# Sorting and summing graph edges in eight column groups, with the stages of neighbouring groups side by side

## The chip, the cores and the metric

The kernel runs on one core of a Trainium2 chip. The metric is device time in microseconds; the kernel before took 3344.22 us (median of three runs, 3344.13 to 3344.76). Less is better.

The engines named here are PE (matrix products), DVE (elementwise work and reductions), ACT (activation functions, copies), POOL (which issues the indirect transfers) and SP (which issues plain transfers). PEld is PE's weight load. ACT can issue plain transfers too.

## The reference

There are 6250 nodes with 128 features and 206250 edges with 128 features. Each edge row is added to its source node; then a small network runs on every node, and a layer norm closes it:

```python
row = edge_index[0]                       # the source node of every edge
edge_aggr = jnp.zeros((n, HIDDEN)).at[row].add(edge_features)
global_expand = jnp.repeat(global_feat, reps, axis=0)
combined = jnp.concatenate([x, edge_aggr, global_expand], axis=-1) @ W_c + b_c
h = jax.nn.softplus(combined @ W1 + b1)
h = jax.nn.softplus(h @ W2 + b2)
return _layernorm(x + (h @ W3 + b3), axis=-1)
```

The source indices come in no useful order, so the sum is a scatter with repeated targets. All values are float32.

## The kernel before

**Layout.** Nodes are cut into blocks of 128; with a node for indices out of range there are `NB` = 49 blocks. Edges are held as 128 partitions by `TC` = 1612 columns: partition p has 1611 consecutive edges, and column 1611 holds the last 42. A bucketed row in DRAM is 129 floats (516 B): the 128 features, and the node's place within its block.

**Sort.** DVE turns the indices into block and place (L126 to L144). For each of the 49 blocks one operation over all columns marks the edges of that block and counts them by partition (L150). Products with a triangle and with ones give each partition's base and the totals (L154, L156). A bucket is padded to whole superchunks of 256 rows. Rows behind the buckets are zeroed by 14 plain transfers (L118) and by 98 indirect ones of 128 rows each (L210, called for `zeros`). Positions follow in groups of 90 columns: a running sum for each block and a predicated copy (L233, L235), then a conversion to integers (L237).

**Scatter.** Nine columns of edge rows at a time are loaded by SP into one of four buffers (L242), ACT adds the place within the block as column 129 (L245), and POOL issues one indirect transfer for each column of 128 rows (L210). There are 1612 of them, into one DRAM tensor `bucketed`.

**Sums.** The sums read `bucketed`, so they begin when every scatter has landed. SP loads eight superchunks at a time (L285). For each 128 rows DVE makes a one-hot matrix (L295) and PE multiplies (L297); after both halves of a superchunk DVE adds the product to the transposed sums at an offset read from `offs` (L300). Each matrix product in float32 shows as two instructions.

**Network.** For 512 nodes at a time: products on PE, softplus in three steps on ACT and two on DVE, the residual, the norm, and the store.

The order of the work on each engine is the framework's: it schedules the instructions by the program's order and by what is ready. The scatters are declared free of order among themselves.

Of the kernel before, what the change touches and what calls it, by code (L numbers as in the profile page):

```python
# [10 lines left out]
U8 = mybir.dt.uint8  # L11
# [7 lines left out]
GROUP_COLS = 90  # L19
SUB = 2  # L20
SC = SUB * P
SC_PER_LOAD = 8
EPS = 1e-5


@with_exitstack
def kernel(
# [24 lines left out]
    # Node N stands for indices out of range, and is no row of the result.  # L52
# [3 lines left out]
    NSC = (E + NB * (SC - 1)) // SC  # L56
    ROWS = NSC * SC
    W = D + 1

    const = ctx.enter_context(tc.tile_pool(name="const", bufs=1))  # L60

# [1 line left out]
    iota_f = const.tile([P, P], F32, name="iota_f")  # L63
    nc.gpsimd.iota(iota_f, pattern=[[1, P]], base=0, channel_multiplier=0,
# [4 lines left out]
    ident = const.tile([P, P], F32, name="ident")  # L69
    nc.vector.tensor_scalar(ident, iota_f, part_f, None, op0=ALU.is_equal)  # L70
    after = const.tile([P, P], F32, name="after")
    nc.vector.tensor_scalar(after, iota_f, part_f, None, op0=ALU.is_gt)
    ones = const.tile([P, P], F32, name="ones")
    nc.vector.memset(ones, 1.0)

    offs = const.tile([1, NSC], I32, name="offs")
    sums_t = const.tile([P, NB * P], F32, name="sums_t")
    nc.gpsimd.memset(sums_t, 0.0)

# [1 line left out]
    wc_sb = const.tile([P, 3, D], F32, name="wc_sb")  # L81
    nc.scalar.dma_start(wc_sb, w_c.rearrange("(k p) d -> p k d", p=P))
    w_sb = {}
    for name, w in (("w1", w1), ("w2", w2), ("w3", w3)):
        w_sb[name] = const.tile([P, D], F32, name=f"{name}_sb")
        nc.scalar.dma_start(w_sb[name], w)
    cols = const.tile([P, 4], F32, name="cols")
    for i, v in enumerate((b_c, b1, b2, global_feat.rearrange("o d -> (o d)"))):
        nc.scalar.dma_start(cols[:, i:i + 1], v.rearrange("(p o) -> p o", o=1))
    b3_row = const.tile([1, D], F32, name="b3_row")  # L90
    nc.scalar.dma_start(b3_row, b3.rearrange("(o d) -> o d", o=1))
    c_bias = const.tile([P, 1], F32, name="c_bias")

    dram = ctx.enter_context(tc.tile_pool(name="dram", bufs=1, space=bass.MemoryType.DRAM))
    bucketed = dram.tile([ROWS + NB * SUB * P, W], F32, name="bucketed")

# [1 line left out]
    with ExitStack() as phase:  # L98
        keep = phase.enter_context(tc.tile_pool(name="keep", bufs=1))
        scans = phase.enter_context(tc.tile_pool(name="scans", bufs=2))  # L100
        rows_p = phase.enter_context(tc.tile_pool(name="rows", bufs=4))
# [3 lines left out]
        if R:  # L105
            nc.vector.memset(src_i[:, T:TC], 0)
        nc.sync.dma_start(src_i[:, :T], src[:P * T].rearrange("(p t) -> p t", p=P))
        if R:
            nc.sync.dma_start(src_i[:R, T:TC], src[P * T:].rearrange("(p o) -> p o", o=1))

        # Rows past the last superchunk that is certainly used.
        ZR = 7
        zeros = keep.tile([P, ZR * W], F32, name="zeros")
        nc.gpsimd.memset(zeros, 0.0)
        tail = (NSC - NB) * SC
        for r0 in range(tail, ROWS, P * ZR):
            k = min(ZR, (ROWS - r0) // P)
            nc.sync.dma_start(  # L118
                bucketed[r0:r0 + P * k, :].rearrange("(p k) c -> p (k c)", p=P),
                zeros[:, :k * W],  # L120
            )

        # Negative indices count from the end; what is out of range goes to node N.
        node = keep.tile([P, TC], F32, name="node", tag="t0")
        wrap = keep.tile([P, TC], F32, name="wrap", tag="t1")
        nc.vector.tensor_copy(node, src_i)  # L126
        nc.vector.tensor_scalar(wrap, node, 0.0, float(N), op0=ALU.is_lt, op1=ALU.mult)
        nc.vector.tensor_add(node, node, wrap)
        nc.vector.tensor_scalar(node, node, -1.0, float(N), op0=ALU.max, op1=ALU.min)
        nc.vector.tensor_scalar(wrap, node, 0.0, float(N + 1), op0=ALU.is_lt, op1=ALU.mult)  # L130
        nc.vector.tensor_add(src_i, node, wrap)
        part_i = keep.tile([P, TC], I32, name="part_i", tag="t1")
        block = keep.tile([P, TC], BF16, name="block")
        nc.vector.tensor_scalar(part_i, src_i, 7, None, op0=ALU.arith_shift_right)
        nc.vector.tensor_copy(block, part_i)
        if R:
            # The last column has R edges.
            none = keep.tile([P, 1], F32, name="none")
# [86 lines left out]
        while g0 < TC:  # L225
            g1 = min(TC, g0 + GROUP_COLS)
            if TC - g1 <= 1:
                g1 = TC
# [158 lines left out]
```

## Time and profile before

| | |
|---|---|
| median of the runs | 3344.22 us |
| span of the profiled execution | 3156.7 us |
| own time of that execution | not listed apart from its span; the runs' median stands for it |
| POOL busy | 1695.3 us (54%) |
| DVE busy | 1161.0 us (37%) |
| PE busy | 716.9 us (23%) |
| ACT busy | 178.2 us (6%) |
| bytes moved | 346.72 MB, 110 GB/s on the mean |

The span runs from the first to the last instruction; the rest of the time lies around it. A profile row of the groups gives line, engine, operation, tiles, shapes and count, then the busy time, the mean duration in ns, and the idle time ahead of it with what ended it. Timeline rows begin with the start and the length in us. A row of a window gives start and end, the length, each engine's busy time with its number of instructions, then PE's granted clock, the mean busy share of the 16 DMA engines and what they moved.

### The profile page before, as it was taken

To read this page: it belongs to the slowest core of one execution; us is meant where nothing else is said; L and a number is where in the kernel's file an instruction comes from. 1 tells how busy PE (TensorE), PEld (TensorE's weight loads), DVE (VectorE), ACT (ScalarE), POOL (GpSimd) and SP (SyncE) were. 2 spreads that over 40 slices of the span, in tenths; PEclk is the share of its full clock that TensorE was granted. 3 is DMA by queue.
4 is the path that set the end of the run, shared out by engine and by line. 5 is a ranking of instruction groups with operands and counts; after the bars stand their busy time and mean duration, and the time that the engine had idled before them with its cause. 6 is when DMAs were issued, how large, how long until landed. Compare 5 with 4: busy or idle time off the path is not lost. (4 is left out here: it accounts for less than half of the span.)

```text
span 3156.7 us, 18596 instructions
## 1 busy us (share of the span) xinstructions
PE 716.9 (23%) x3776; PEld 527.9 (17%) x3776; DVE 1161.0 (37%) x4793; ACT 178.2 (6%) x368; POOL 1695.3 (54%) x1720
## 2 busy tenths in 40 slices
PE   0000000000000000000000000000049999999885
PEld 0000000000000000000000000000037777777543
DVE  9999995000000000000000000000029999999644
ACT  0000000000000000000000000000000000000267
POOL 1577777777777777777777777777730000000000
PEclk9999999999999999999999999999999999999965
DMA  3012333333333333333333333333356565656200
GB/s 128 15 48 71 97 98 103 103 101 104 104 105 105 104 105 104 105 105 105 104 105 104 105 105 105 104 103 102 102 156 188 176 187 177 185 178 185 68 16 24
DMA packets 386717, 346.72 MB, mean 110 GB/s; under 512 B 33101, under 2 KB 355802, under 8 KB 386602
## 3 DMA queue, kind: packets, MB, share of 16 engines
q1 hardware_dynamic: 328812, 228.93, 25.8%
q0 software_dynamic: 54720, 113.01, 11.0%
q10 hardware_dynamic: 3070, 3.60, 0.4%
q14 instruction: 85, 0.70, 0.1%
q8 instruction: 30, 0.49, 0.1%
HBM read 222.83 MB, written 122.57 MB: 109 GB/s over the span
## 5 line engine op out<-in xcount | busy, mean ns | idle before, releaser
L210 POOL DMA_INDIRECT bucketed<-rows,pos x1612 | 1562.0, 969 | 491.6 <-issue 489.4
L297 PE MATMUL part<-hot,chunks 128*128 128x128 f32 x3416 | 569.9, 302 | 2273.1 <-DVE hot L295 2246.5
L295 DVE TENSOR_SCALAR hot<-iota_f,chunks 128x128 f32<-128x128 f32 x1708 | 406.7, 280 | 1818.5 <-DMA chunks<-bucketed 1812.8
L297 PEld LDWEIGHTS part<-hot,chunks 128*128 128x128 f32 x3416 | 448.2, 191 | 2394.1 <-issue 2213.6
L233 DVE TENSOR_TENSOR_SCAN scan<-ones,scan,in_block 128x90 f32<-128x90 f32 (+1 forms) x833 | 323.1, 389 | 0.0
L300 DVE TENSOR_TENSOR sums_t<-sums_t,part 128x128 f32 x854 | 245.4, 287 | 63.2 <-PE part L297 34.9
L235 DVE COPY_PREDICATED pos_f<-in_block,scan 128x90 f32<-128x90 uint8 (+1 forms) x882 | 200.0, 228 | 0.0
L210 POOL DMA_INDIRECT bucketed<-zeros,pad_i x98 | 124.0, 1266 | 132.5 <-DVE pos_f L235 103.3
L245 ACT COPY rows<-low 128x9 f32<-128x9 f32 x179 | 36.6, 206 | 2230.0 <-DMA bucketed<-rows,pos 2219.4
L150 DVE TENSOR_SCALAR_CACHE_REDUCE in_block<-block 128x1612 uint8<-128x1612 bf16 x49 | 85.9, 1821 | 0.0
L329 ACT ACTIVATE comb<-comb_ps,c_bias 128x512 f32<-128x512 f32 (+1 forms) x13 | 8.4, 646 | 617.4 <-PE comb_ps L326 617.4
L340 PE MATMUL y_ps<-w_sb,h 128*128 128x128 f32 (+1 forms) x98 | 33.2, 437 | 26.1 <-DVE h L313 25.6
L341 PE MATMUL y_ps<-b_row,ones 1*128 1x128 f32 (+1 forms) x98 | 35.6, 459 | 0.0
L340 PEld LDWEIGHTS y_ps<-w_sb,h 128*128 128x128 f32 (+1 forms) x98 | 24.6, 291 | 53.5 <-DVE h L313 36.4
L310 ACT ACT_TABLE_LOAD x26 | 33.4, 1283 | 0.5
L313 DVE TENSOR_TENSOR h<-h,away 128x512 f32<-128x512 f32 (+1 forms) x26 | 17.1, 656 | 37.5 <-ACT away L310 37.5
L318 PE MATMUL z_ps<-h,w_sb 128*128 128x512 f32 (+1 forms) x26 | 22.8, 976 | 9.3 <-DVE h L313 9.3
L154 PE MATMUL before_ps<-count,after 128*128 128x49 f32 x2 | 0.7, 432 | 106.7 <-DVE in_block L150 106.7
L342 DVE TENSOR_TENSOR y<-y_ps,x_sb 128x128 f32<-128x128 f32 (+1 forms) x49 | 13.8, 285 | 29.6 <-PE y_ps L341 29.6
L309 ACT ACT_TABLE_LOAD x19 | 24.4, 1283 | 0.3
L341 PEld LDWEIGHTS y_ps<-b_row,ones 1*128 1x128 f32 (+1 forms) x98 | 22.1, 279 | 9.9 <-issue 8.5
L312 DVE TENSOR_SCALAR h<-z_ps,cols 128x512 f32<-128x512 f32 (+1 forms) x26 | 18.2, 707 | 14.7 <-ACT away L308 14.7
(85 smaller groups left out, 284.8 us busy)
## 6 DMA issues: line engine op xcount, KB each, us to landing
chunks<-bucketed SPq DMA_DIRECT2D x106, 1032.0 KB, 5.3
rows<-in_edge_attr SPq DMA_DIRECT2D x179, 576.0 KB, 4.6
bucketed<-rows,pos POOLq DMA_INDIRECT x1612, 2.4
bucketed<-zeros SPq DMA_DIRECT2D x14, 451.5 KB, 8.7
out<-y SPq DMA_DIRECT2D x12, 256.0 KB, 2.2
bucketed<-zeros,pad_i POOLq DMA_INDIRECT x98, 2.4
src_i<-in_src SPq DMA_DIRECT2D x1, 805.5 KB
chunks<-bucketed SPq DMA_DIRECT2D x1, 774.0 KB
```

The lines of the kernel that those rows point to most:

```text
L150: nc.vector.tensor_scalar(in_block[:, b, :], block, float(b), None, op0=ALU.is_equal, op1=ALU.add, accum_out=count[:, b:b + 1])
L210: s = nc.gpsimd.indirect_dma_start(out=bucketed[:, :], out_offset=bass.IndirectOffsetOnAxis(ap=index, axis=0), in_=rows, in_offset=None)
L233: nc.vector.tensor_tensor_scan(scan[:, b, :n], ones[:, :n], in_block[:, b, g0:g1], first, op0=ALU.mult, op1=ALU.add)
L235: nc.vector.copy_predicated(pos_f[:, g0:g1], in_block[:, b, g0:g1], scan[:, b, :n])
L245: nc.scalar.copy(rows[:, :k, D:W], low[:, c0:c0 + k].unsqueeze(2))
L295: nc.vector.tensor_scalar(hot, iota_f, chunks[:, s, j, D:W], None, op0=ALU.is_equal)
L297: nc.tensor.matmul(part, chunks[:, s, j, :D], hot, start=(j == 0), stop=(j == SUB - 1))
L300: nc.vector.tensor_add(here, here, part)
L309: nc.scalar.activation(away[:, :w], away[:, :w], AF.Exp, scale=-1.0)
L310: nc.scalar.activation(away[:, :w], away[:, :w], AF.Ln, bias=ones[:, :1])
L340: nc.tensor.matmul(y_ps[:r, :], h2[:, q0:q0 + r], w_sb["w3"], start=True, stop=False)
L341: nc.tensor.matmul(y_ps[:r, :], ones[:1, :r], b3_row, start=False, stop=True)
```

## The change

The 1612 columns are cut into eight groups of 64, 192, 384, 384, 288, 144, 92 and 64 columns. Each group has its own counts, positions, buckets and offsets. Buckets are padded to 128 rows (groups 0, 6 and 7) or to 256 (the others).

Three DRAM tensors, `places`, take the buckets: group 0 has its own, and the others alternate between two. Each tensor is filled once with -1; a row's last column now holds `1 + 128 * group + place in block`, so that a row left by an earlier group or by the fill matches no node of the present one. The indirect transfers of zero rows are gone.

In the main loop, for each group: its scatters, the positions of the next group, and the sums of the group before are written out in turn, piece by piece, and the order on PE, DVE, ACT and SP is the written one. Edge rows are loaded through ACT's queue three pieces ahead, into one of five buffers. Fills, row transfers for the positions, chunk loads and x go through SP's queue.

Positions are found in another way: a comparison of all columns of a part with all blocks at once in bfloat16; counts by products with ones; the base of each column as a bfloat16 pair of high and low byte, moved from partitions into one row by SP; a product with a triangle plus a product with the base row; then a multiplication by the comparison and a reduction over the 49 blocks. The one-hot matrices for 1024 rows are made by one operation, on rows loaded 1024 at a time. The MLP loads x again on ACT's queue, 512 nodes at a time; the transposes of x lie in the loop, in group 2.

The core of the diff:

```diff
+GROUPS = ((64, 1), (192, 2), (384, 2), (384, 2), (288, 2), (144, 2), (92, 1), (64, 1))
+CHUNK_ROWS = 1024
+FILL = 12
+POS_COLS = 8
+ROW_COLS = 64
...
+    rows_of = [nsc * sub * P for _, _, sub, nsc in groups]
+    place_rows = [rows_of[0]] + [max(rows_of[1 + i::2], default=0) for i in range(2)]
+    places = [dram.tile([r, W], F32, name=f"place{i}") for i, r in enumerate(place_rows) if r]
+    place_of = [0 if g == 0 else 1 + (g - 1) % 2 for g in range(G)]
...
+        rows_p = phase.enter_context(tc.tile_pool(name="rows", bufs=5))
+        chunks_p = phase.enter_context(tc.tile_pool(name="chunks", bufs=4))
+        hots = phase.enter_context(tc.tile_pool(name="hots", bufs=2))
...
+        def fill_rows(place, r0, r1):
+            for r in range(r0, r1, P * FILL):
+                k = min(FILL, (r1 - r) // P)
                 nc.sync.dma_start(
+                    places[place][r:r + P * k, :].rearrange("(p k) c -> p (k c)", p=P),
+                    fill[:, :k * W])
...
+            def count(k):
+                a, b = parts[k]
+                n = b - a
+                ib = hots_p.tile([P, P, NB], BF16, name="ib")
+                in_block[k] = ib
+                nc.vector.tensor_tensor(
+                    ib[:, :n, :], block[:, a:b].unsqueeze(2).to_broadcast([P, n, NB]),
+                    iota_h[:, :NB].unsqueeze(1).to_broadcast([P, n, NB]), op=ALU.is_equal)
+
+            def count2(k):
+                n = parts[k][1] - parts[k][0]
+                n_ps = ps.tile([P, NB], F32, name="n_ps")
+                for b in range(NB):
+                    nc.tensor.matmul(n_ps[:n, b:b + 1], in_block[k][:, :n, b], ones_h[:, :1],
+                                     start=True, stop=True)
+                nc.scalar.copy(n_all[:n, k, :], n_ps[:n, :])
...
+            def one_row(k, r0):
+                r1 = min(parts[k][1] - parts[k][0], r0 + ROW_COLS)
+                row = per.tile([2, ROW_COLS * NB], BF16, name="gb_row")
+                gb_row[k, r0] = row
+                for h in range(2):
+                    nc.sync.dma_start(row[h:h + 1, :(r1 - r0) * NB], got[k][r0:r1, h, :])
+
+            def place(k, j0, j1):
...
+                nc.tensor.matmul(pr[:, :m * NB], after_h, ib, start=True, stop=False)
+                r0 = j0 // ROW_COLS * ROW_COLS
+                nc.tensor.matmul(pr[:, :m * NB], scale_h,
+                                 gb_row[k, r0][:, (j0 - r0) * NB:(j1 - r0) * NB],
+                                 start=False, stop=True)
...
+            def place2(k, j0, j1):
...
+                nc.vector.tensor_mul(at[:, :m * NB], pr[:, :m * NB], ib)
...
+                    nc.vector.tensor_reduce(
+                        pos[:, a - c0 + j0:a - c0 + j1],
+                        at[:, :m * NB].rearrange("p (g b) -> p g b", b=NB),
+                        axis=mybir.AxisListType.X, op=ALU.add)
...
+            def load(i):
...
+                nc.sync.dma_start(
+                    t[:, :k * sub].rearrange("p (s j) c -> p s (j c)", j=sub),
+                    src_rows[s * sub * P:(s + k) * sub * P, :].rearrange(
+                        "(s p j) c -> p s (j c)", p=P, j=sub))
+
+            def match(i):
...
+                nc.vector.tensor_tensor(
+                    hot[:, :m], chunks[i][:, :m, D:W].to_broadcast([P, m, P]),
+                    code.unsqueeze(1).to_broadcast([P, m, P]), op=ALU.is_equal)
+
+            def total(i):
...
+                for s in range(k):
+                    part = ps.tile([P, P], F32, name="part", bufs=3)
+                    for j in range(sub):
+                        nc.tensor.matmul(part, t[:, s * sub + j, :D], hot[:, s * sub + j],
+                                         start=(j == 0), stop=(j == sub - 1))
+                    here = sums_t[:, bass.ds(at[s], P)]
+                    nc.vector.tensor_add(here, here, part)
...
+        with tc.manual_schedule(engines={ET.PE, ET.DVE, ET.Activation, ET.SP}):
...
+            fill_rows(0, 0, rows_of[0])
...
+            for step in positions(0):
+                step()
+            if G > 1:
+                fill_rows(1, 0, rows_of[1])
...
+            for g in range(G):
+                mine = [q for q in range(len(pieces)) if pieces[q][0] == g]
+                prep = positions(g + 1) if g + 1 < G else []
+                sums = reduce_steps(g - 1) if g else []
+                other = node_rows() if g == min(2, G - 1) else []
+                if g == 0 and G > 2:
+                    fill_rows(1, rows_of[1], place_rows[1])
+                if g == 1 and G > 2:
+                    fill_rows(2, 0, place_rows[2])
+                done = [0, 0, 0]
+                for q in mine:
+                    load_rows(i + 3)
+                    code_rows(i + 2)
+                    scatter_rows(i)
...
+                    for w, (todo, s) in enumerate(((prep, min(1.0, share * 1.15)), (sums, share),
+                                                   (other, share))):
+                        upto = int(round(len(todo) * s))
+                        for step in todo[done[w]:upto]:
+                            step()
+                        done[w] = upto
+            for step in reduce_steps(G - 1):
+                step()
...
+        x_sb = node_rows_of(work, nc.scalar, n0, w)
```

More of the change, by code (lines that the diff above doesn't have):

```diff
@@ L87 @@
     cols = const.tile([P, 4], F32, name="cols")
[L88 to L89 removed]
     b3_row = const.tile([1, D], F32, name="b3_row")
[L91 to L95, printed above, removed]
+    x_t = const.tile([P, N], F32, name="x_t")
@@ L114 @@
[L114 to L127, printed above, removed]
@@ L209, in scatter @@
-        def scatter(rows, index):
-            s = nc.gpsimd.indirect_dma_start(
-                out=bucketed[:, :], out_offset=bass.IndirectOffsetOnAxis(ap=index, axis=0),
-                in_=rows, in_offset=None)
-            tc.declare_no_dep(s.ins, group="scatter", reason="no two edges have one position")
-            tc.add_to_no_dep_group("scatter", s.ins)
-        for b in range(NB):
-            for k in range(SUB):
-                scatter(zeros[:, :W], pad_i[:, b, k:k + 1])
-        pos_f = keep.tile([P, TC], F32, name="pos_f", tag="t0")
```

454 lines of the change are left out of this document (284 added, 170 removed).

## The prediction

> **What bounds the kernel now.** I read the page's slices first, then busy times in windows cut at the stage borders, then the timeline at those borders. From the page:
>
> ```profile
> span 3156.7 us, 18596 instructions
> ...
> DVE  9999995000000000000000000000029999999644
> ...
> POOL 1577777777777777777777777777730000000000
> ...
> L210 POOL DMA_INDIRECT bucketed<-rows,pos x1612 | 1562.0, 969 | 491.6 <-issue 489.4
> ```
>
> POOL works alone in the middle, DVE (with PE) before and after: three stages in a row. The windows price them (columns: window, length, busy time and count of PE, weight loads, DVE, ACT, POOL, clock, DMA share, GB/s):
>
> ```profile
> 0.00:36.00 36.00, 0.00 (x0) 0.00 (x0) 29.57 (x34) 1.79 (x5) 9.26 (x10) 1.00 0.84 280
> 36.00:112.00 76.00, 3.02 (x7) 1.29 (x8) 74.54 (x103) 0.00 (x0) 0.00 (x0) 1.00 0.00 0
> 112.00:267.00 155.00, 2.10 (x5) 0.63 (x3) 154.78 (x674) 0.00 (x0) 124.26 (x99) 1.00 0.13 42
> 267.00:520.00 253.00, 0.00 (x0) 0.00 (x0) 251.92 (x1110) 4.13 (x20) 196.60 (x186) 1.00 0.34 96
> 520.00:2321.00 1801.00, 0.00 (x0) 0.00 (x0) 0.00 (x0) 32.16 (x156) 1365.20 (x1427) 1.00 0.36 103
> 2321.00:2334.00 13.00, 5.80 (x28) 5.83 (x29) 4.82 (x22) 0.02 (x1) 0.00 (x0) 1.00 0.92 270
> 2334.00:2969.00 635.00, 572.46 (x3443) 449.88 (x3442) 562.48 (x2540) 7.07 (x13) 0.00 (x0) 0.99 0.59 178
> 2969.00:3157.00 188.00, 133.51 (x299) 70.30 (x297) 82.91 (x313) 132.99 (x173) 0.00 (x0) 0.64 0.06 17
> ```
>
> 112 us of indices and counts, 155 us of padding scatters, 2054 us (267 to 2321) of 1612 edge scatters, 648 us of sums (2321 to 2969), 188 us of MLP. A scatter starts every 1801/1427 = 1.262 us while DVE rests and every 253/186 = 1.360 us beside a full DVE. Its gap is "issue": POOL waits for nothing, so its own work per scatter is the pace.
>
> **The sum's frame.** Outside the span lie 3344.2 - 3156.7 = 187.5 us, taken from the median, since the execution shown has no time but its span; the three runs lie within 0.6 us, so it matters little. I keep that part unchanged.
>
> **What stays on the path.** All 1612 edge scatters stay on POOL, one after another. Removed: the 98 padding scatters (155 us) and most of the 112 us ahead of them. Moved beside the scatters: sums of seven groups and positions of seven groups. Left behind the last scatter: sums of group 7, then the MLP.
>
> **First scatter: 33 us.** A group's place has (columns*128 + 49*(128*sub - 1))/(128*sub) chunks; group 0, with 64 columns and sub 1, has 112, that is 14336 rows of 516 B, 7.4 MB of filling. The nearest row for fills, and those for the small operations:
>
> ```profile
> 25.00:30.00 5.00, 0.00 (x0) 0.00 (x0) 5.00 (x7) 0.00 (x0) 0.00 (x0) 1.00 1.02 395
> ```
> ```profile
> L204 PEld LDWEIGHTS ended<-chunk_f,ones 49*1 49x1 f32 x4 | 0.3, 101 | 2.8 <-issue 1.5 <-DVE chunk_f L200 1.3
> L128 DVE TENSOR_TENSOR node<-node,wrap 128x1612 f32<-128x1612 f32 x1 | 1.8, 1836 | 0.0
> L188 DVE TENSOR_TENSOR spare<-spare,pad_f 128x98 f32<-128x98 f32 x1 | 0.3, 253 | 0.0
> ```
> ```profile
> 6.13 1.95 DVE L126 CAST node<-src_i 128x1612 f32<-128x1612 int32 x1 [5.12 <-DMA src_i<-in_src]
> ...
> 107.12 0.63 PE L156 MATMUL total_ps<-count,ones 128*128 128x49 f32 x2
> ...
> 109.58 0.19 DVE L172 SCALAR_TENSOR_TENSOR base<-start,before_ps 128x49 f32<-128x49 f32 x1
> ```
>
> Fill, indices and first rows, some 10 MB at 395 GB/s, take 25 us; issue and start bring them to about 30. In parallel: indices at 6 us, eleven small DVE operations at about 0.2 (between L188's 0.25 and overlap) 2.5, the comparison of 64*49 = 3136 elements at 1836/1612 = 1.14 ns 3.6, 49 weight loads with products at 0.1 to 0.2 about 7, totals and bases 3 (107.12 to 109.77), the row transfer behind the fill, first products and position 3. Both meet near 33 us. Bounds 25 to 50.
>
> **Group 1 waits for a queue: +32 us.** After group 0's row transfers SP issues the fill of the whole of place 1, 61440 rows or 31.7 MB, and only then group 1's row transfers, which positions(1) needs. At 395 GB/s that is 80 us. The 64 scatters run meanwhile (64*1.262 = 81 us) at a DMA share of 0.36 (row 520 to 2321), so the queue is through after 80 + 0.36*81 = 109 us, about 7 more (an estimate: 2.3 to land, as 2319.15 to 2321.40 below, the rest a first product, multiplication and reduction): group 1 starts at 33 + 109 + 7 = 149 us against 33 + 84 without the wait. No row has fill and scatter together: from no wait (117) to the fill at 178 GB/s, the rate of the sums' stage (211). Place 2's fill (31.7 MB again) and group 0's sums lie in group 1's 262 us, which covers 109 + 14 loads. The index work of the other 1548 columns, about 20 us of DVE by the 13 us it took for all columns at once (6.13 to 19), lies beside group 0's scatters; so do the weights on ACT's queue. The 13 transposes of x move into group 2, which has the most room.
>
> **1548 further scatters at 1.262 = 1954 us.** A shared cost comes on top. Beside a busy DVE the starts fall into step:
>
> ```profile
> 265.31 0.40 DVE L233 TENSOR_TENSOR_SCAN scan<-ones,scan,in_block 128x90 f32<-128x90 f32 x1
> 265.40 1.07 POOL L210 DMA_INDIRECT bucketed<-zeros,pad_i  x1 [0.30 <-issue]
> 265.63 0.23 DVE L235 COPY_PREDICATED pos_f<-in_block,scan 128x90 f32<-128x90 uint8 x1
> 265.77 0.39 DVE L233 TENSOR_TENSOR_SCAN scan<-ones,scan,in_block 128x90 f32<-128x90 f32 x1
> ...
> 266.77 1.07 POOL L210 DMA_INDIRECT bucketed<-rows,pos  x1 [0.30 <-issue]
> ...
> 268.15 1.07 POOL L210 DMA_INDIRECT bucketed<-rows,pos  x1 [0.30 <-issue]
> ```
>
> 1.37 us is three times DVE's cycle of 0.46 us (265.31 to 265.77): at some point a scatter waits for a DVE operation with two SBUF operands to end. If it can begin anywhere in an operation of d us, one operation costs d*d/(2*1.262). Scan (0.31) and copy (0.15) would cost 0.047 us per 0.46 us, 0.128 per scatter; measured is 1.360 - 1.262 = 0.098, three quarters. Now the new operations with two SBUF operands: `match`, 1024 elements, 1.17 us by L128, and the group comparisons, up to 6272 elements, 7.1 us. There are 286,208 place rows (14336 + 36864 + 61440 + 61440 + 49152 + 30720 + 17920 + 14336), so 280 matches: 280*1.17*1.17/2.52 = 152 us. Of a long comparison all but half a pitch is lost: 1612*49*1.14 ns = 90 us in 15 pieces, 80. With index work 215 in all is 0.75 of that about **160 us**. Bounds: 0 (only scans do it) and every such microsecond, 328 + 90 = 418. I take 160 as the trace's own factor.
>
> [...]
>
> **Are the moved stages covered?** Prices:
>
> ```profile
> L297 PE MATMUL part<-hot,chunks 128*128 128x128 f32 x3416 | 569.9, 302 | 2273.1 <-DVE hot L295 2246.5
> ...
> L300 DVE TENSOR_TENSOR sums_t<-sums_t,part 128x128 f32 x854 | 245.4, 287 | 63.2 <-PE part L297 34.9
> ```
>
> Before, 128 rows cost 635/1708 = 0.372 us with PE and DVE both near full. At that price group g-1's sums need 42, 107, 179, 179, 143, 89, 52 us inside groups 1 to 7 of 262, 524, 524, 393, 197, 126, 87 us (columns times 1.365): the tightest, group 5, is 73% full on PE. DVE there: 48 matches at 1.17, 192 additions at 0.29, positions of 92 columns (two more passes of 49 elements a column beside the comparison, 0.17 us a column): 130 of 197. DMA there: 0.36 + 25.4 MB/197 us = 129 GB/s at 0.59/178, together 0.79. So all fit. POOL is not in front of them, but what holds them holds it: ACT issues row loads behind the copies of counts, SP issues chunk loads and row transfers in one order, and a group's first load waits for the last scatter before it. Three pieces of rows are loaded ahead, 34 us. I give six later borders 3 us each: **18** (0 to 60).
>
> **Tail.** Last scatter to first addition:
>
> ```profile
> 2319.15 0.90 POOL L210 DMA_INDIRECT bucketed<-rows,pos  x1 [0.31 <-issue]
> 2321.40 19.27 SPq L285 DMA_DIRECT2D chunks<-bucketed  x5
> ...
> 2327.81 1.48 DVE L295 TENSOR_SCALAR hot<-iota_f,chunks 128x128 f32<-128x128 f32 x7 [1808.86 <-DMA chunks<-bucketed]
> ```
>
> ```profile
> 0.74 0.47 ACTq L82 DMA_DIRECT2D wc_sb<-in_L_gnn_W_c  x1
> ```
>
> 2.3 + 6.4 us, then 14 loads of eight chunks: PE 8*0.372 = 3.0, with hand-over 3.5: 49. Together **57** (45 to 90). The MLP keeps its 188 us; 14 issues of x on ACT at 0.47 us, an engine busy 133 of the 188, make it **195** (clock 0.64 or better: 170 to 215).
>
> **Sum:** 149 + 1954 + 160 + 18 + 57 + 195 = 2533, with 187.5 outside **2720 us**, 18.7% less. All low ends give 2473, all high ends 3140.
>
> **Rivals.**
> *Every locked microsecond is lost*, since matches, comparisons and scatters take turns: 2720 - 160 + 418 = 2978. [...]
> *Nothing collides*: no lock loss, no fill wait, no border cost: 2720 - 160 - 32 - 18 = 2510. For it: POOL waits for no DMA now. Against it: the 1.37 us steps.
> *The second fill also holds up work*: positions(2) and sums of group 0 come behind place 2's fill in SP's queue; if fills get half of what I assume, 262 us do not cover it and some 130 us are lost: 2850. For it: one queue, in order; against it: 395 GB/s.
> *The change does not overlap*: a wait between groups leaves sums behind scatters: 33 + 1612*1.262 + 2236*0.372 + 195 + 187.5 = 3282. The places alternate, which speaks against.
> *Slower than before*: the scatters' packets queue behind chunk, row and fill packets on the 16 DMA engines until POOL cannot hand over the next. It decides from 2720 + 624 = 3344, that is 0.40 us on each of 1548 scatters, a pitch of 1.77 us; at 2.0 us 3700. Against it: shares of 0.36 and 0.59 hardly add to one, as the sums run at under half density.
>
> **How the numbers follow.** Forecast 0.68 (own range 2590 to 2860), turns 0.09, no collision 0.10, second fill 0.06, no overlap 0.03, slower 0.04. From 2500 to 2980 all but the last two and thin edges lie inside. Runs of this kernel tell 0.2%, 7 us, from no change; of the case without overlap 0.01 goes to no change. Faster 0.95, same 0.01, slower 0.04.
>
> **What would show it.** POOL in one block from near 33 us with a gap of about 30 us before scatter 65; 1.26 us between scatters where DVE runs sums_t additions and 1.3 to 1.5 where it matches; PE busy in all middle slices; about 57 us from the last scatter to the first `comb_ps`. A pitch above 1.5 us, or gaps at group borders over 20 us, would make the prediction wrong.

## The result and the profile after

The changed kernel takes 3235.49 us (median of four runs, 3225.67 to 3261.45), the kernel before beside it 3344.49 (3344.13 to 3348.99): a ratio of 0.9677, 95% interval 0.9637 to 0.9718. It is faster by 3.2%, where 18.7% were forecast; 2720 with its range of 2500 to 2980 is missed by 515 us.

**The same two programs take two pairs of times.** In some comparisons the kernel before takes 3158 to 3166 us, in others 3344 to 3353, each repeated within 0.3%. The first is called P here (signals are prompt), the second L (signals come late; the runs below show it). The time in front of the prediction, and those just given, are from L; the profile before, with its span of 3156.7 us, is from P. PE's granted clock doesn't tell them apart: for the kernel before its mean is 0.973 to 0.977 under P and 0.974 to 0.979 under L. What makes an execution the one or the other is not known. Comparisons below stay within one of the two.

The page of the changed kernel (under L) answers to the rows of before:

```profile
span 3230.3 us, 22159 instructions
...
PE   1140116423242402032325721134761373557875
...
POOL 4447760476656867656672577745057506450000
...
L434 POOL DMA_INDIRECT place<-rows,pos x1612 | 1626.3, 1009 | 1255.0 <-ACT rows L426 569.2
L356 PE MATMUL part<-hot,chunks 128*128 128x128 f32 x4472 | 858.6, 351 | 990.5 <-issue 700.9
L359 DVE TENSOR_TENSOR sums_t<-sums_t,part 128x128 f32 x1300 | 372.8, 287 | 1513.9 <-remote 1018.4
L343 DVE TENSOR_TENSOR hot<-chunks,iota_f 128x1024 f32<-128x1024 f32 (+1 forms) x280 | 340.3, 1217 | 99.3 <-DMA chunks<-place 77.7
```

POOL no longer works in one block: the forecast had it at seven tenths in all of the middle slices, and here stand 0, 2 and many 4 to 6. Its own time is nearly as before (1009 ns against 969), a match takes 1.22 us for 1.17 forecast, a product 351 ns for 302 at a lower granted clock (0.69 on the mean for 0.98), so no instruction has grown enough to make up 515 us. What is new are 569 us in which POOL waits for a code of a piece of rows from ACT, and 1018 us in which DVE's additions wait for "remote", that is, for a signal ahead of which the profile finds no work of this core. The view of waits gives their number and the longest (us in total, times, longest):

```profile
DVE sums_t L359 <- remote: 1018.4, 153, 25.5
ACT n_all L202 <- PE n_ps L200: 751.1, 11, 167.8
...
POOL place L434 <- ACT rows L426: 569.2, 18, 123.8
```

The timeline shows such a wait of DVE by itself, where no scatter is issued (start, length, engine, operation, idle time ahead):

```profile
482.23 0.50 PE L258 MATMUL pr<-gb_row,scale_h 2*128 2x392 bf16 x1
...
486.59 0.57 DVE L269 TENSOR_TENSOR at<-pr,ib 128x392 f32<-128x392 f32 x1 [4.24 <-remote]
...
487.63 0.50 PE L258 MATMUL pr<-gb_row,scale_h 2*128 2x392 bf16 x1
...
492.19 0.57 DVE L269 TENSOR_TENSOR at<-pr,ib 128x392 f32<-128x392 f32 x1 [4.44 <-remote]
```

The product has ended at 488.1 and DVE, which has nothing else to do, starts at 492.2. The last scatters had been issued at 476.9, after a stretch of 192 without a gap. Two windows of the same trace show what it costs (columns as before): the first beside scatters, the second in a gap of POOL.

```profile
380.00:480.00 100.00, 14.71 (x41) 8.48 (x42) 9.86 (x23) 1.23 (x6) 73.73 (x77) 1.00 0.36 104
...
500.00:600.00 100.00, 73.37 (x309) 49.32 (x308) 85.70 (x182) 0.20 (x1) 0.00 (x0) 0.69 0.23 59
```

Counted from the trace's records of PE's signals: 283 of the 1351 recorded ahead of the network come over 0.5 us behind the end of their product, 1467 us in sum, all beside scatters or within some 25 us of them. Below, "late" is this count. The trace lacks a record for 119 of the 1470 signals sent there, so a second count does without records. It takes how long each of the 1300 additions starts behind the end of both its product and DVE's instruction before it: 253 start over 0.5 us late, 1353 us in sum.

### The profile page after: what moved, and what is told of

Same layout as the page of the kernel before. It is cut to its first block, busy times and chain, and to the rows that moved or that the text cites. A ratio compares the mean times of both kernels' runs of the same rounds, so it can differ in the third digit from the quotient of the medians.

```text
span 3230.3 us, 22159 instructions
## 1 busy us (share of the span) xinstructions
PE 1226.6 (38%) x6078; PEld 915.4 (28%) x6078; DVE 1115.3 (35%) x2549; ACT 181.2 (6%) x386; POOL 1633.3 (51%) x1620
## 4 chain that ended last, share of the span: by engine, by line
another core or an unknown queue 31%; issue 24%; DVE 15%; PE 15%; POOL 6%; DMA 5%; ACT 2%; DVEq 1%; SPq 1%; ACTq 0%; POOLq 0%
PE part L356 9%; DVE sums_t L359 7%; POOL place L434 6%; DMA place<-rows,pos 2%; DVE at L269 2%; DVE pos L271 2%; DVE hot L343 2%; DVE ib L192 1%; DMA rows<-in_edge_attr 1%; PE y_ps L541 1%; PE z_ps L518 1%; PE y_ps L540 1%; PE n_ps L200 1%; DVEq L359 1%
## 5 line engine op out<-in xcount | busy, mean ns | idle before, releaser
L434 POOL DMA_INDIRECT place<-rows,pos x1612 | 1626.3, 1009 | 1255.0 <-ACT rows L426 569.2
L356 PE MATMUL part<-hot,chunks 128*128 128x128 f32 x4472 | 858.6, 351 | 990.5 <-issue 700.9
L356 PEld LDWEIGHTS part<-hot,chunks 128*128 128x128 f32 x4472 | 731.1, 245 | 1130.6 <-issue 773.3
L359 DVE TENSOR_TENSOR sums_t<-sums_t,part 128x128 f32 x1300 | 372.8, 287 | 1513.9 <-remote 1018.4
L343 DVE TENSOR_TENSOR hot<-chunks,iota_f 128x1024 f32<-128x1024 f32 (+1 forms) x280 | 340.3, 1217 | 99.3 <-DMA chunks<-place 77.7
L256 PE MATMUL pr<-ib,after_h 128*128 128x392 bf16 x202 | 87.2, 432 | 468.7 <-DVE at L269 306.1
L269 DVE TENSOR_TENSOR at<-pr,ib 128x392 f32<-128x392 f32 x202 | 112.6, 558 | 235.2 <-issue 117.5
L258 PE MATMUL pr<-gb_row,scale_h 2*128 2x392 bf16 x202 | 88.0, 436 | 238.0 <-DMA gb_row<-half_h 121.4
L271 DVE TENSOR_REDUCE pos<-at 128x8 int32<-128x392 f32 x202 | 113.2, 560 | 7.0
L192 DVE TENSOR_TENSOR ib<-block,iota_h 128x6272 bf16<-128x6272 bf16 (+4 forms) x16 | 84.0, 5292 | 0.0
```

What stands on the lines that cost most here:

```text
L192: nc.vector.tensor_tensor(ib[:, :n, :], block[:, a:b].unsqueeze(2).to_broadcast([P, n, NB]), iota_h[:, :NB].unsqueeze(1).to_broadcast([P, ...
L256: nc.tensor.matmul(pr[:, :m * NB], after_h, ib, start=True, stop=False)
L258: nc.tensor.matmul(pr[:, :m * NB], scale_h, gb_row[k, r0][:, (j0 - r0) * NB:(j1 - r0) * NB], start=False, stop=True)
L269: nc.vector.tensor_mul(at[:, :m * NB], pr[:, :m * NB], ib)
L271: nc.vector.tensor_reduce(pos[:, a - c0 + j0:a - c0 + j1], at[:, :m * NB].rearrange("p (g b) -> p g b", b=NB), axis=mybir.AxisListType.X, ...
L343: nc.vector.tensor_tensor(hot[:, :m], chunks[i][:, :m, D:W].to_broadcast([P, m, P]), code.unsqueeze(1).to_broadcast([P, m, P]), op=ALU.is_ ...
```

## The experiments

The first theories, A and B, were formed on this trace, before the two conditions were known. A: signals of PE are late wherever POOL scatters. B: the order on each engine (ACT's copy of counts ahead of its row loads) makes the gaps, whatever POOL does.

**The kernel before once more.**

> The kernel before, unchanged, profiled once more. The prediction kept 187.5 us outside the span as a constant (3344.2 less a span of 3156.7); the changed kernel's profiled execution has 3232.3 us and a span of 3230.3, so 2.0 us outside. If the 187.5 us are a cost of launching that the changed kernel lost, this run shows a span near 3157 and a time near 3344 again. If the span of the first profile simply belongs to an execution that took another time than the median, this run shows a span within some 5 us of its own time, and no 187.5 us lie outside anything.

```profile
span 3160.3 us, 18596 instructions
```

Its time is 3162.06 us, 1.8 us above its span. So no 187.5 us lie outside the span; later comparisons under L list spans of 3342 to 3351 us beside times 1.8 us longer. Five more profiles of this kernel were taken beside other runs in the hope of seeing it under L; all came out at 3158 to 3162, under P. What was expected of the last stands for all:

> The kernel before, once more, for the condition in which it takes 3345 us. Backlog: its first scatters 1.26 to 1.29 us apart, from some hundreds of us on 1.38, all 184 us between first and last scatter, none in the sums. At 3160 us it repeats the first profile, and where the 184 us lie stays open.

So the stage in which the kernel before loses 184 us under L has not been seen.

**Without scatters.**

```diff
-            for j in range(k):
+            for j in range(0):
```

> The changed kernel with the 1612 edge scatters left out (the places keep what the filling wrote, so the sums of the edges are not computed); all positions, loads of chunks, matches, products and additions still run, in the same order on PE, DVE, ACT and SP. Theory A (signals of PE reach DVE late while POOL scatters, about 5 us on each hand-over): with no scatters no hand-over is late, the additions wait under 1 us for their product, eight groups of positions and sums take about 1000 to 1300 us in all and the whole under 1600 us. Theory B (the order of the work on each engine, one waiting for the other, makes the gaps, whatever POOL does): the count copies on ACT and the additions on DVE keep waits of the same sizes, some 750 us before the count copies and 1000 us before the additions, and the whole stays over 2000 us.

It took 1744 us (P, one run). The waits, us in total, times, longest:

```profile
ACT n_all L202 <- PE n_ps L200: 779.4, 16, 156.2
...
DVE sums_t L359 <- PE part L356: 95.1, 142, 7.7
```

No signal is late, but ACT's copies of counts wait as long as ever: that wait is in the order of the program and needs no late signal. The time lies between the two forecasts; since P has no late signals with scatters either, the run doesn't decide.

**Without sums.**

```diff
-                sums = reduce_steps(g - 1) if g else []
+                sums = []
```

> The changed kernel with the sums of all eight groups left out: no chunks are loaded, matched, multiplied or added (the sums of the edges stay zero); fills, positions and scatters stay. Theory A: positions still have a hand-over from PE to DVE for each eight columns, about 202 in all, each late by some 4 to 6 us beside the scatters (some 900 us in a span of 2000), but they start at once, so that they mostly stay ahead of the scatters: POOL's block ends near 2100 to 2300 us, the whole at 2300 to 2500, and waits of about 5 us for PE are still there before the multiplications of the positions. Theory B: without the sums between them the positions have nothing to queue behind, so the waits before the multiplications fall below 1 us and POOL has no gap over 10 us after scatter 65.

2388 us (P, one run), no late signal, and from scatter 65 on no gap over 1 us: 1548 scatters in 2022 us. Taken apart, that is 68 us by which single scatters are longer than usual, and 1.262 us for each, the pitch of before.

**The copy of counts on DVE.**

```diff
-                nc.scalar.copy(n_all[:n, k, :], n_ps[:n, :])
+                nc.vector.tensor_copy(n_all[:n, k, :], n_ps[:n, :])
```

> The copy of the counts of 128 columns moved from ACT to DVE, so that loads of rows and their codes on ACT no longer queue behind a product of PE. Theory B (this queueing is the cause of POOL's 569 us behind the codes): the block of scatters closes up, the whole at about 2700 us. Theory A (late signals make positions and sums slower than the scatters): the wait only moves, POOL then waits for positions or DVE instead, and the gain is under 200 us: 3030 to 3240.

2805 us (P, one run), which could only be read beside the next run: it is 90 slower than the changed kernel under P. DVE now waits 40 us for PE's products of the counts (9 times), and POOL's gaps from scatter 65 on are 244 us in place of 160. Theory B in this form has fallen.

**The changed kernel under P.**

> The changed kernel, unchanged, profiled and timed once more beside the kernel before. The comparison of the prediction had the kernel before at 3344 us; the first group of experiments had it at 3160 with the same program, and there the version with the copy of counts on DVE had not one product whose signal came late, where the first profile of the changed kernel had 285 late by over 0.5 us, 1485 us in sum. Theory A as first put (late signals belong to scatters beside products, always): 3200 to 3260 us again with some 280 late signals, and the 2805 us of the other version is due to the moved copy. Theory A2 (the late signals are a condition of the chip at that time, the one that also gave the kernel before 3344): beside a kernel before at 3160 there are no late signals here and the time is 2750 to 2900; beside a kernel before at 3344 it is 3230 again.

2714.40 us (2710.76 to 2720.65), the kernel before 3161.81: 0.8587 (0.8568 to 0.8606). Not one signal is late, and 2 of the 1300 additions start over 0.5 us late, by 0.6 each. So theory A fell as first put, A2 stood. The page and three rows of waits:

```profile
span 2711.1 us, 22159 instructions
...
POOL 4657775377777877777777677777457717730000
...
L434 POOL DMA_INDIRECT place<-rows,pos x1612 | 1677.0, 1040 | 716.4 <-issue 469.2
L359 DVE TENSOR_TENSOR sums_t<-sums_t,part 128x128 f32 x1300 | 372.3, 286 | 295.3 <-PE part L356 200.4
```
```profile
ACT n_all L202 <- PE n_ps L200: 488.8, 14, 97.0
...
PE pr L258 <- DMA gb_row<-half_h: 255.1, 7, 117.7
...
POOL place L434 <- ACT rows L426: 162.2, 4, 56.3
```

At the place of the timeline above, and beside scatters, DVE goes from one position step to the next in 1.06 us, without idle time, where it took 5.6:

```profile
454.88 0.56 DVE L269 TENSOR_TENSOR at<-pr,ib 128x392 f32<-128x392 f32 x1
...
455.55 0.96 POOL L434 DMA_INDIRECT place<-rows,pos  x1 [0.30 <-DVE at L269]
...
455.94 0.56 DVE L269 TENSOR_TENSOR at<-pr,ib 128x392 f32<-128x392 f32 x1
```

Three gaps of POOL over 10 us are left, 56, 43 and 53 us (152 of 160), each three pieces into a group (2, 5 and 6). At the second:

```profile
1980.18 0.20 ACT L202 CAST n_all<-n_ps 92x49 bf16<-92x49 f32 x1 [88.46 <-PE n_ps L200]
...
1981.45 0.96 POOL L434 DMA_INDIRECT place<-rows,pos  x1 [43.13 <-ACT rows L426]
```

ACT stands 88 us before its copy; POOL has pieces loaded ahead for 45 of them. PE comes late to the counts because the sums ahead of them in its order are late: those of groups 3, 4 and 5 end at 1966, 2216 and 2377 us, while the scatters beside them end at 1899, 2135 and 2314. And the sums are late although DVE has time; by the trace, they can't run ahead of POOL:

```profile
SPq L333 <- DMA rows<-in_edge_attr: 903.2, 57, 91.5
```

In the first trace of the changed kernel the 450 transfers of SP and the 208 of ACT signal their end on eight counters, 82 or 83 on each, and 281 of SP's stand behind a wait for the counter that they signal on. Chunk loads on SP so wait for row loads on ACT, which wait for row buffers, which wait for scatters. That this makes the sums late is read from the trace; no run took it away alone.

**The order of the queues.** Copies on DVE, loads of x on ACT, place 2 filled in pieces all along group 1, the rest of place 1 in group 2:

```diff
-                    fill_rows(1, rows_of[1], place_rows[1])
-                    fill_rows(2, 0, place_rows[2])
+                    fills = fill_steps(2, 0, place_rows[2])
+                if g == 2:
+                    fills = fill_steps(1, rows_of[1], place_rows[1])
```

> Edits in the order of the queues alone: the copy of counts and the copy of the turned x on DVE in place of ACT, the loads of x for them on ACT's queue in place of SP's, the rest of place 1 filled in group 2 in place of group 0, and place 2 filled in pieces along group 1 in place of all at its start. If the gaps of POOL come from SP's and ACT's order (fills ahead of the row transfers of positions; loads of rows behind copies that wait for PE), the gap before scatter 65 falls from 49 to about 20 us, that before scatter 320 (74) goes, and it takes 2650 to 2730 us beside a kernel before at 3160. If they come from late signals of PE, it takes within 100 us of the changed kernel.

2790.27 us, 0.8821 (0.8806 to 0.8835), P: 76 slower than the changed kernel, and 14 faster than the one run with the copies on DVE, which it contains. Against that run the gap before scatter 65 fell from 49 to 18 us as expected, and the one before scatter 320 (74) went. But the filling, now issued piece by piece between the sums' loads, ended too late: 83 us before scatter 257, where there were 15. Most of what SP's order gave was paid back there.

**Copies of counts later in ACT's order.**

```diff
             steps.append(lambda: count2(len(parts) - 1))
+            steps.extend([lambda: None] * (LATER if g else 0))
+            for k in range(len(parts)):
+                steps.append(lambda k=k: count3(k))
```

> The changed kernel with one edit of ACT's order: the copies of a group's counts come some four pieces of rows later in the order than the products that make them (one PSUM tile holds the counts of all parts, so that PE goes on), so that four more loads of rows and their codes stand ahead of them on ACT. Where the kernel before takes 3160 us, the changed kernel took 2714, with gaps of POOL of 56, 43 and 53 us that ended with a copy of counts on ACT, three pieces into a group. If these gaps come from row loads that queue behind a copy which waits for a late product, they fall below 15 us in sum and the time to 2560 to 2600. If POOL would then only wait for something else that is late (the positions of the next group, which now start later), it stays within 50 us of 2714. Beside a kernel before at 3344 signals of PE come late again, and it takes 3000 to 3250.

2701.27 us, 0.8551 (0.8537 to 0.8566), P: 13 us less than the changed kernel, the second answer and not the first. The gaps moved (29 before scatter 65, then 52, 18, 43 and 32) and did not shrink: behind scatter 65 they are 164 us for 160. That fits a cause in PE's late work, behind which it matters little which wait ends last; it doesn't prove it.

**A bench for the hand-over.** PE and DVE pass a tile to and fro, 6 rounds beside each nine scatters; the sums are left out.

```diff
+                    pong = ps.tile([P, P], F32, name="part", bufs=3)
+                    nc.tensor.matmul(pong, ident, ping, start=True, stop=True)
+                    nc.vector.tensor_copy(ping, pong)
```

> A bench for the hand-over from PE to DVE, in the changed kernel with the sums of all groups left out (the sums of the edges stay zero) and put in their place: a chain in which PE multiplies what DVE copied last and DVE copies what PE multiplied last, 6 rounds beside each nine scatters in groups 2, 3 and 4. In group 2 nothing else is added; in group 3 SP issues 10, in group 4 30 transfers of 512 B beside each nine scatters, each with as many completion signals as any other transfer; behind the last scatter 60 rounds alone, then 60 beside 300 such transfers. If a heavy traffic of completion signals is what makes PE's signals late, rounds take 1.0 to 1.5 us in group 2 and alone, and grow by several us in groups 3 and 4 (5 us a round as in the first profile of the changed kernel, or more). If the traffic does not matter where the kernel before takes 3160 us, rounds take within 0.2 us of the same time in all five stretches, and the late signals stay bound to the one comparison with the kernel before at 3344.

This run met L (before 3345.82). It took 4027 us. PE ran ahead of POOL, so that even the rounds meant to be alone had scatters beside them, and the small transfers made the scatters slower, which was not meant either and became the finding. Two windows and DVE's longest wait in each, first in group 2, then in group 3:

```profile
560.00:1050.00 490.00, 233.12 (x661) 134.41 (x661) 119.96 (x345) 14.87 (x50) 309.49 (x324) 1.00 0.36 95
1200.00:1800.00 600.00, 167.28 (x425) 94.02 (x425) 86.86 (x252) 7.01 (x34) 299.52 (x313) 1.00 0.65 69
```
```profile
DVE ping L484 <- remote: 183.4, 38, 10.1
```
```profile
DVE ping L484 <- PE part L483: 466.7, 115, 139.0
```

In group 2 a scatter comes every 490/324 = 1.51 us on the mean, in runs of 27 (median) at 1.26: rounds take 1.18 us in the median, and 183 us go to waits for "remote", the longest 10.1. In group 3 one comes every 600/313 = 1.92 us, in runs of 4: no such wait, though small transfers add their completions; if each makes 16, 16 a us are due there and 13 in group 2 (the first profile of the kernel before has 16 for each of its 1710 scatters, 27360 in all, and 16 for each of three loads of 512 B). So the mean number of completions is not the cause. The pace of the scatters over some tens of us might be: that made theories C (backlog) and D (touch) of the next runs.

**Fillings spread over part of group 1**, on top of the later copies:

```diff
+                    fills, quick = fill_steps(2, 0, place_rows[2]), 1.7
```

> The version with the later copies of counts (2701 us), and in it the filling of place 2 spread over the first six tenths of group 1 in place of all at its start, and the rest of place 1 filled along group 2 in place of ahead of group 1's positions. The wait of 52 us that was left three pieces into group 2 ended with a product of PE that stood behind positions, whose row transfers stood behind the filling in SP's queue. If that queue is the cause, this gap and half of the one before scatter 65 (29 us) go: 2630 to 2660. If the filling now ends too late for group 2's first scatter, as in the version that spread it over the whole of group 1 (a gap of 83 us before scatter 257), it takes 2700 or more.

It met L beside the bench: 3205.10 us, 0.9593 (0.9558 to 0.9627), with 335 late signals, so it said nothing on SP's queue. A second try, with the last pair below, met L again: 3209.37, 0.9587 (0.9562 to 0.9613). Under P it was never run.

**Scatters made slower.** A memset of 128x256 on POOL behind each one (POOL's order is then the written one too):

```diff
                 tc.add_to_no_dep_group("scatter", s.ins)
+                nc.gpsimd.memset(idle, 0.0)
```

> The changed kernel with one small instruction of POOL (a memset of 128x256, some 0.22 us) behind each edge scatter, so that scatters start about every 1.5 us and not every 1.26. Two theories of the late signals on the chip that gives the kernel before 3345 us. Backlog: there the completions of the scatters drain at no more than one scatter per 1.38 us (1.262 plus 184 us over 1612 scatters); scatters that start faster pile up a backlog, and PE's signals stand in it. Then at 1.5 us hardly a signal is late (under 30 by over 0.5 us, where 285 were), and the time there falls from 3235 to 2900 to 3050 although POOL does more. Touch: any scatter under way delays signals, whatever their rate. Then 200 or more stay late and it takes 3250 to 3500. On a chip that gives the kernel before 3160 us no signal is late in either theory and it takes 2714 plus some 0.15 to 0.25 us for each of 1612 scatters, less the gaps it fills: 2850 to 3100.

It met P: 2892.68 us, 0.9153 (0.9137 to 0.9170), as both theories had it. The memset took 0.33 us on the mean, for some 0.22 expected; a scatter starts every 1.56 us, and POOL's wait for ACT falls from 162 us to

```profile
POOL place L434 <- ACT rows L426: 19.4, 2, 13.2
```

so at that pace positions and sums nearly keep up. With this memset in groups 3 to 7 only, and one of 128x1, which leaves the pitch at 1.26, in groups 0 to 2:

> The changed kernel with a small instruction of POOL behind each scatter: a memset of 128x256 in groups 3 to 7, of 128x1 in groups 0 to 2 (which leaves the distance between scatters near 1.26 us there), so that one run holds both paces. On a chip that gives the kernel before 3345 us, backlog expects late signals in groups 1 and 2 as ever (80 or more by over 0.5 us up to about 1150 us) and, from some 50 us after group 3 begins, hardly any (under 15), a pitch of about 1.46 to 1.6 there, and 2950 to 3100 us in all. Touch expects late signals in all groups alike, and over 3235 us. On a chip that gives 3160 us: no late signal, the gaps of POOL in the first groups as in the changed kernel and next to none from group 3 on, and 2780 to 2870 us.

2831 us (P, one run): gaps of 26 and 56 us in the groups at the old pace, and 21 in the others.

**The deciding pair**, the version with later copies and spread fillings, with the memset and without:

> The version with later copies of counts and spread fillings, and behind each of its scatters the memset of 128x256 on POOL, so that scatters start every 1.46 us or more. On the chip that gives the kernel before 3345 us this version without the memset took 3205 us with 335 late signals of PE: backlog expects fewer than 30 late signals and 2800 to 2950 us, touch some 300 and over 3205. On a chip that gives 3160 us there is no late signal, and it takes 40 + 1612 x 1.56 for the scatters, some 100 for the sums behind them and 200 for the MLP: 2830 to 2890.

> The version with later copies of counts and spread fillings, which so far ran only where the kernel before takes 3345 us. Where that takes 3160, it is 2630 to 2660 if SP's queue made the wait of 52 us three pieces into group 2, and 2700 or more if the filling now ends too late for group 2's first scatter. At 3345 us it repeats 3205.

Both met L (before 3348.82). Without the memset 3209 us; its waits:

```profile
DVE sums_t L372 <- remote: 1085.5, 152, 30.7
```

With it 2892 us (one run, 0.864 of the kernel before), though POOL is busy for 652 us more (2274.6 for 1622.4); its page, and the same wait:

```profile
span 2890.2 us, 23796 instructions
...
POOL 4898885988888988888888888888888899890000
```
```profile
DVE sums_t L372 <- remote: 6.8, 4, 3.2
```

Late signals ahead of the network: 309 of 1326 recorded without, 38 of 1166 with, 1711 and 48 us in sum. Records are missing in both, so the count without records decides: 259 of 1300 additions start over 0.5 us late without (1498 us) and 23 with (25 us). Touch expected some 300 late signals and over 3205 us. It has fallen; backlog is what no run contradicts. The memset costs the changed kernel 178 us under P, and saves this version 317 under L.

The same link shows inside the traces without the memset. Where 35 or more scatters start in the 50 us ahead of a product's end, which is one every 1.43 us or faster, 113 of 114 signals are late in the version without the memset and 96 of 101 in the first profile of the changed kernel; where fewer than 5 start, 1 of 362 and none of 460.

A size fits in part. 184 us over 1612 scatters make 1.262 + 0.114 = 1.38 us, the pace that the kernel before seems to be held to. If a scatter is taken to occupy something for that time, and the queue is counted forward through the trace without the memset, more than two scatters stand in it at 123 of the 309 late signals and at none of the 1017 prompt ones; at 1.44 us, at 176 and 24. So such a queue leaves many late signals unexplained. This is a count on one trace, not a run of its own.

## Why the prediction was wrong

The working can be laid beside the same program in both conditions. Borders are those of the trace; "gaps" are those over 1 us behind scatter 65, "longer scatters" what those of over 1.1 us take beyond 0.96, and the row of 1548 scatters is what these two leave of the time from scatter 65 to the last.

| term | forecast | P, 2712.9 us | L, 3232.3 us |
|---|---|---|---|
| start of group 1 | 149 | 161.7 | 165.9 |
| 1548 scatters at 1.262 | 1954 | 1953.6 | 1952.2 |
| lock: longer scatters | 160 | 125.5 | 76.1 |
| borders: gaps | 18 | 160.2 | 694.7 |
| last scatter to the network | 57 | 107.7 | 137.8 |
| network | 195 | 202.4 | 203.6 |
| outside the span | 187.5 | 1.8 | 2.0 |
| sum | 2720 | 2712.9 | 3232.3 |

**The step that failed is the price of the cover**, "I give six later borders 3 us each": 18 us, with a bound of 60, against 694.7, and against 160.2 where no signal is late. The prediction had the coupling ("what holds them holds it: ACT issues row loads behind the copies of counts"), and priced the moved stages by a hand-over that it had only seen with POOL idle. Under L a late hand-over beside scatters costs 2.7 us in the median and up to 32; the additions alone wait 1018 us for it, and ACT, then POOL, wait behind PE and DVE. Under P the 160 us come from the order of the work and its queues, as far as the trace tells: moving the copies of counts alone left 164, and no run untied the two queues. No row of the profile before could show this: there PE and POOL never work together beyond a few products.

**The frame failed too.** 187.5 us "outside the span" are nothing of the kind: 3344.2 and 3156.7 belong to two conditions. A span 6% below a median that repeats within 0.02% was itself the sign that the profile shows another condition than the times, and "I keep that part unchanged" was the wrong answer to it. That 2714 under P lies at 2720 is no success: the working without this term is 2533, and 180 us that it lacks, most of them in gaps and tail, happen to fill it. That is luck.

**First scatter** 39.7 us for 33. **Group 1** starts at 166 for 149; the gap ahead of it, behind the filling, is 24 us for 32.

**The pitch was right**: between undisturbed scatters 1.263 us in the median under P and 1.266 under L, for 1.262. **So was the lock**, a scatter's wait for an operation of DVE to end, **in kind and, under P, nearly in size.** There:

```profile
1640.48 1.22 DVE L343 TENSOR_TENSOR hot<-chunks,iota_f 128x1024 f32<-128x1024 f32 x1
1640.52 2.00 POOL L434 DMA_INDIRECT place<-rows,pos  x1 [0.30 <-issue]
...
1642.83 0.96 POOL L434 DMA_INDIRECT place<-rows,pos  x1 [0.30 <-issue]
```

A scatter that comes 0.04 us behind the start of a match takes 2.00 us in place of 0.96, and ends 0.82 behind the match's end: nearly all of it runs when the match is over. Over the whole program matches cost the scatters 77 us (three quarters of 152, so 114, in the working), the group comparisons 50 (60), and the 1300 additions, which read one operand from PSUM, 5. The working added 152 and 80 to 215, where they make 232; three quarters of that are 174 and not 160, a slip of 14 us that changes nothing here. That only operations with two SBUF operands hold up a scatter was the author's assumption; these three sums agree with it, and no run tested it by itself. Turns in full, 418, are not seen: 120 of the 280 matches hold up a scatter by over 0.14 us, 0.64 us each on the mean.

**Tail**: 57 us were for group 7 alone. Its 14 loads take 51 us from first to last match, as forecast, but group 6's sums were still to do, since the cover had not held: 107.7 under P, 137.8 under L. **The network**: 203 for 195.

**The rivals.** *No collision* and *turns* fell by the lock's rows. *The second fill* is real but small: under P PE waits 255 us for row transfers (the row of `gb_row` above), most of them behind the filling, and by the trace this is one of the causes of the 56 us gap; the runs that were to test it met L. *No overlap* (3282) is nearest in time under L and wrong in kind: sums do run beside scatters. *Slower through packets* had a pitch of 1.77; it stayed 1.263 to 1.266.

## What to carry to other kernels

Before a span is subtracted from a median, see that both come from the same condition; a difference of 6% is a finding, not a constant. A stage that is moved beside another can pay for each hand-over under the new neighbour (here 2.7 us in the median of the late ones under L, while none came late under P), so count its hand-overs between engines, not only its busy time, and bound them by what nothing has shown yet. Where work is paced by scatters, an issue rate that the rest can follow may beat the fastest one: 0.2 us more between scatters took 317 us off under L.

## What the runs showed of the hardware

Signals from PE to DVE came 2.7 to 3.3 us late in the median of the late ones, and up to 32, while POOL issued scatters of 128 rows every 1.26 us, and for up to 25 us more: 283 of 1351 recorded in the changed kernel, 309 of 1326 with later copies and spread fillings. With the memset behind each scatter, which makes 1.46 us of the 1.26, 38 of 1166 did. Ten transfers more by SP beside each nine scatters brought no wait for "remote" in the bench, where a scatter came every 1.92 us. Late signals were seen under L only; the changed kernel under P had none. Whether L belongs to a chip, to an hour or to something else that differs between executions is open: chips are told by a number alone, and one number showed both. What backs up is open as well.

Under L the trace itself lacks records: it holds 3763 of scatter completions in the first profile of the changed kernel and 18193 with the memset, for 25776 under P. What became of the others no run shows. Each run here lists a span and a clock from its records, so none can tell whether late signals are a cost of recording; that rival is untested.

No version was seen to be best in both conditions: 2701 us (P) is the one with later copies, 2892 (L) the one with the memset as well as later copies and spread fillings. The changed kernel with the memset alone takes 2893 under P.
